# A graph network in four layers: the scores' R as two float32r rows, spread in one pass; both sides' scores from one product

## The chip, the cores and the metric

The kernel runs on one core of a Trainium2 chip. The metric is the device time of one execution, in microseconds (us). Before the change it was 3072.85 us, the median of three executions (3069.26 to 3073.18).

The engines are named as in the profile: PE (matrix products; PEld is its weight load), DVE (vector), ACT (scalar functions), POOL (here: gathers by index), SP (issues transfers).

## The reference

Four layers over N = 3327 nodes of width D = 512; each reads a normed copy of x and adds its result to x. Layers 0, 2 and 3 are graph attention with H = 8 heads of F = 64, layer 1 takes the mean over neighbours.

```python
h = jnp.maximum(_layernorm(x, axis=-1), 0.0);  x = x + L0(h, adj)   # likewise L1, L2, L3

def attention(h, adj, W, a):             # L3; L0 adds a batch norm and relu, L2 has own a1, a2
    hp = jnp.einsum('nd,hdf->hnf', h, W)
    f_src = jnp.einsum('hnf,hf->hn', hp, a_src)
    f_dst = jnp.einsum('hnf,hf->hn', hp, a_dst)
    e = jax.nn.leaky_relu(f_src[:, :, None] + f_dst[:, None, :], 0.2)
    att = jax.nn.softmax(jnp.where(adj[None] > 0, e, -9e15), axis=-1)
    return elu(jnp.einsum('hij,hjf->hif', att, hp))       # heads side by side

def sage(h, adj, ...):                   # L1
    agg = (adj > 0) @ h / jnp.maximum(deg, 1.0)
    return relu(concat([h @ W_self + b, agg @ W_nb + b], -1) @ W_comb + b_comb)
```

The adjacency is sparse: an edge has a probability of about half a per cent, more for the first nodes.

The kernel uses that exp(leaky_relu(s + d)) is exp(d) times exp(0.2 s) times the larger of exp(0.8 s) and exp(-0.8 d). The middle factor falls out of the softmax. So a target node i needs only R(i) = exp(0.8 s_i), per head, scaled by a constant, and a neighbour j needs exp(d_j), exp(-0.8 d_j) and its row of hp.

## The kernel before

**Tiling.** The nodes are padded to 26 blocks of 128 rows. The targets are taken in 52 groups of 64 (GB), ordered by the nodes' index; each group has a list of its neighbours in chunks of 128: 22 chunks for the first group, 4 for the last, 359 in all (21 of the groups have five). Work of attention goes in units of up to three chunks (UNIT = 3), of the averaging layer in parts of two.

**Stages**, with their place in the profiled execution:
- 0 to 330 us: the lists are made from the adjacency, and beside them the projection of layer 0, block by block (`Projection.block`, L578-604). Here the scheduler chooses the order.
- 330 to 400: list transfers.
- 400 to 980: attention of layer 0, with products of weights for layer 1 beside it (fwx, bmean, fb).
- 980 to 1155: batch norm, layer 1's own products.
- 1155 to 1757: averaging (SAGE); beside it the projection of layer 2, by `Following`.
- 1757 to 2462: attention of layer 2; beside it the projection of layer 3, by `Following`.
- 2462 to 3068: attention of layer 3, with no projection.

**A projection** makes, for each block of 128 nodes: the transposed block hT; the scores s and d of all heads; hp = h W (wh). It leaves two things in memory: a row per node in `table` (V: exp(d) times hp and exp(d) itself, then exp(-0.8 d)), and R in `r_dram`, with the nodes along the row. WA holds the attention vectors already multiplied into W, for a side H = 8 columns: the first 8 for s, the next 8 for d. Before the change d comes from hT as the stationary operand (L708 in `Following`: 128 nodes by 8), and s from WA as the stationary operand (L710: 8 by 128 nodes), so that s comes out along the row. Each is four products, over the four parts of D.

`Following.rest` (L698-731) is a generator. Its steps for a block: transposes p_ps (L701) and hT by ACT (L704) | both score products p_sd (L708, L710), the exps of d (L713, L714), the copy of s out of PSUM (L716) | the clamp on DVE (L719), the products p_wh (L722) | the exp of R on ACT (L724), its transfer (L726), V's eight scalings (L730), the transfer of the table's rows (L731). `Following.tick` (L661) advances the first ready block by one step, and the blocks still in their norm by one each. A tick is called once per unit in attention, and once per pair of chunks in SAGE (L1320-1360). The tiles p_ps, p_sd and p_wh share one tag in PSUM, with two buffers during SAGE and one during attention 2 (`pb`).

**Attention** (`attend`, L1000-1125) has its order on PE, DVE and ACT written out by hand: each engine runs its instructions in the order of the program. For each group R's row is fetched two groups ahead (L1017-1020, a transfer of 512 values to one partition), and spread one group ahead: `spread` (L1023-1028) multiplies a column of ones with it, so that all 128 partitions have the 64 x 8 values (r_bc, one bank of PSUM). For each unit: DVE takes the larger of r_bc and the gathered exp(-0.8 d) (mx, L1096), DVE multiplies by the mask (wgt, L1103), the rows of the next unit are gathered (POOL, L995), `later()` runs a step of the endings of earlier groups and the tick (L1062), then at the start of a group the spread of the next, then PE's 8 products per chunk (facc, L1117). The ending of a group copies the sums (L1045), and scales the heads (rd L1049, fhp L1055); every second one finishes a block (fin_e, fin_x).

All data is float32, and a float32 product is issued as two records of matmul in the trace.

Of the kernel before, what the change touches and what calls it, by code (L numbers as in the profile page):

```python
# [22 lines left out]

F32 = mybir.dt.float32
BF16 = mybir.dt.bfloat16
I32 = mybir.dt.int32
I8 = mybir.dt.int8
U8 = mybir.dt.uint8
U16 = mybir.dt.uint16
AF = mybir.ActivationFunctionType  # L30
ALU = mybir.AluOpType
# [5 lines left out]
P = 128  # L37
H = 8
F = 64
D = H * F  # L40
KC = D // P
# [7 lines left out]
GB = 64  # L49
# [10 lines left out]
SMALL = 53.0  # L60
# [502 lines left out]
class Projection:  # L563
# [15 lines left out]
    def block(self, c):  # L579
        nc, pp, pps, WA, wl = self.tc.nc, self.pool, self.psum, self.WA, self.wl  # L580
        hT = self.norms.block(c, self.hs)
        wh = pps.tile([P, D], F32, name="wh_ps", tag="wh_ps", bufs=1)
        sd = pps.tile([P, BANK], F32, name="sd_ps", tag="sd_ps", bufs=1)
        for kc in range(KC):
            nc.tensor.matmul(sd[:, :H], hT[:, kc, :], WA[:, wl, kc, H:], start=(kc == 0), stop=(kc == KC - 1))
        for kc in range(KC):
            nc.tensor.matmul(sd[:H, P : 2 * P], WA[:, wl, kc, :H], hT[:, kc, :], start=(kc == 0), stop=(kc == KC - 1))
        for kc in range(KC):
            nc.tensor.matmul(wh, hT[:, kc, :], self.Wt[:, kc, :], start=(kc == 0), stop=(kc == KC - 1))  # L589
        row = pp.tile([P, ROW], F32, name="v_row", tag="v_row", bufs=3)  # L590
        V = row[:, : H * (F + 1)].rearrange("p (h f) -> p h f", f=F + 1)
        nc.scalar.activation(V[:, :, F : F + 1], sd[:, :H].rearrange("p (h o) -> p h o", o=1), AF.Exp)
        nc.scalar.activation(row[:, H * (F + 1) :], sd[:, :H], AF.Exp, scale=-0.8, bias=self.cs["down"])

        rr = pp.tile([H, P], F32, name="r_row", tag="r_row", bufs=2)
        nc.vector.tensor_scalar(rr, sd[:H, P : 2 * P], -SMALL, SMALL, ALU.max, ALU.min)
        nc.scalar.activation(rr, rr, AF.Exp, scale=0.8, bias=self.cs["down"][:H])
        n = P // GB
        nc.sync.dma_start(
            self.r_dram[c * n : (c + 1) * n, :, :].rearrange("g h i -> h g i"), rr.rearrange("h (g i) -> h g i", i=GB)  # L600
        )
        for h in range(H):
            nc.scalar.mul(V[:, h, 0:F], wh[:, h * F : (h + 1) * F], V[:, h, F : F + 1])
        nc.sync.dma_start(self.table[c * P : (c + 1) * P, :ROW], row.bitcast(I32))

# [36 lines left out]
    return step  # L642


class Following:


# [11 lines left out]
        self.early.append(self.norm(c, xt))  # L659

    def tick(self):  # L661
        if self.ready and next(self.ready[0], None) is None:
            self.ready.pop(0)
        for g in list(self.early):
            hx = next(g)
            if hx is not None:
                self.early.remove(g)
                self.ready.append(self.rest(*hx))
# [28 lines left out]
    def rest(self, c, hx):  # L697
        nc, pp, WA, wl = self.tc.nc, self.pool, self.WA, self.wl  # L698
        tp = self.psum.tile([P, KC, P], F32, name="p_ps", tag="p_ps", bufs=self.pb)
        for kc in range(KC):  # L700
            nc.tensor.transpose(tp[:, kc, :], hx[:, kc * P : (kc + 1) * P], self.cs["ident"])  # L701
        hT = pp.tile([P, KC, P], F32, name="hT", tag="hT", bufs=2)
        for kc in range(KC):
            nc.scalar.activation(hT[:, kc, :], tp[:, kc, :], AF.Relu, accum_out=self.hs[:, c, kc : kc + 1])  # L704
        yield True
        sd = self.psum.tile([P, BANK], F32, name="p_sd", tag="p_ps", bufs=self.pb)
        for kc in range(KC):
            nc.tensor.matmul(sd[:, :H], hT[:, kc, :], WA[:, wl, kc, H:], start=(kc == 0), stop=(kc == KC - 1))  # L708
        for kc in range(KC):
            nc.tensor.matmul(sd[:H, P : 2 * P], WA[:, wl, kc, :H], hT[:, kc, :], start=(kc == 0), stop=(kc == KC - 1))  # L710
        row = pp.tile([P, ROW], F32, name="v_row", tag="v_row", bufs=2)
        V = row[:, : H * (F + 1)].rearrange("p (h f) -> p h f", f=F + 1)
        nc.scalar.activation(V[:, :, F : F + 1], sd[:, :H].rearrange("p (h o) -> p h o", o=1), AF.Exp)  # L713
        nc.scalar.activation(row[:, H * (F + 1) :], sd[:, :H], AF.Exp, scale=-0.8, bias=self.cs["down"])  # L714
        rr = pp.tile([H, P], F32, name="r_row", tag="r_row", bufs=2)
        nc.scalar.copy(rr, sd[:H, P : 2 * P])  # L716
        yield True

        nc.vector.tensor_scalar(rr, rr, -SMALL, SMALL, ALU.max, ALU.min)  # L719
        wh = self.psum.tile([P, D], F32, name="p_wh", tag="p_ps", bufs=self.pb)  # L720
        for kc in range(KC):
            nc.tensor.matmul(wh, hT[:, kc, :], self.Wt[:, kc, :], start=(kc == 0), stop=(kc == KC - 1))  # L722
        yield True
        nc.scalar.activation(rr, rr, AF.Exp, scale=0.8, bias=self.cs["down"][:H])  # L724
        n = P // GB
        nc.sync.dma_start(  # L726
            self.r_dram[c * n : (c + 1) * n, :, :].rearrange("g h i -> h g i"), rr.rearrange("h (g i) -> h g i", i=GB)
        )
        for h in range(H):
            nc.scalar.mul(V[:, h, 0:F], wh[:, h * F : (h + 1) * F], V[:, h, F : F + 1])  # L730
        nc.sync.dma_start(self.table[c * P : (c + 1) * P, :ROW], row.bitcast(I32))  # L731
        yield None


# [232 lines left out]
def sparse(ctx: ExitStack, tc: tile.TileContext, t: dict, out: bass.AP, WA, ls, cs, idx, rdeg, first):  # L967
# [5 lines left out]
    nc = tc.nc  # L973
# [9 lines left out]
    dram = ctx.enter_context(tc.tile_pool(name="fdram", bufs=1, space=DRAM))  # L983
# [4 lines left out]
    ones = cs["ones"]  # L988
# [11 lines left out]
    def attend(layer, table, r_dram, finish, tick=lambda: None, home=None):  # L1000
# [11 lines left out]
        with tc.tile_pool(name=f"fatt{layer}", bufs=2) as ap, tc.tile_pool(  # L1012
            name=f"facc_ps{layer}", bufs=2, space=PSUM
        ) as aps, tc.manual_schedule(engines={ET.PE, ET.DVE, ET.Activation}):
            rows, rrs, rbs, accs, ends = {}, {}, {}, {}, []

            def fetch(g):  # L1017
                if g < ls.G:
                    rr = ap.tile([1, H * GB], F32, name="r_one", tag="r_one", bufs=3)
                    nc.sync.dma_start(rr, r_dram[g : g + 1, :, :].rearrange("g h i -> g (h i)"))  # L1020
                    rrs[g] = rr

            def spread(g):  # L1023


                if g < ls.G:
                    rb = aps.tile([P, H * GB], F32, name="r_bc", tag="r_bc", bufs=2)
                    nc.tensor.matmul(rb, ones[0:1, :], rrs.pop(g), start=True, stop=True)  # L1028
                    rbs[g] = rb.rearrange("p (h i) -> p h i", i=GB)

            def ending(g, hps={}):
# [59 lines left out]
            for i, (g, k0, n, begins, stops) in enumerate(units):  # L1091
# [20 lines left out]
                for k in range(n):  # L1112
                    f, l = begins and k == 0, stops and k == n - 1
                    for q in range(hq):
                        for v in range(PG):
                            h = q * PG + v
# [12 lines left out]
    def following(lx, layer, wl, W, pb=1):  # L1129

        table = dram.tile([NP, ROW], I32, name=f"table{layer}")
        r_dram = dram.tile([ls.G, H, GB], F32, name=f"r_dram{layer}")
        pp = lx.enter_context(tc.tile_pool(name=f"fproj{layer}", bufs=1))
        pps = lx.enter_context(tc.tile_pool(name=f"fproj_ps{layer}", bufs=1, space=PSUM))
        return Following(tc, cs, N, wl, W, WA, table, r_dram, pp, pps, pb)
# [24 lines left out]
    with ExitStack() as mx:  # L1160
# [180 lines left out]
        for i, (b, _, begins, stops) in enumerate(parts):  # L1341
# [4 lines left out]
            for r, u, k, m, z in loaded.pop(i):  # L1346
# [3 lines left out]
                g = b * PG + u  # L1350
# [17 lines left out]
def gnn_stack(tc: tile.TileContext, t: dict, out: bass.AP):  # L1368
    with ExitStack() as ctx:

        tc.nc.scalar.preload_act_table_set("natural_log_exp_and_others")
        WA, ok = products(ctx, tc, t)
        N, NP = out.shape[0], t["x"].shape[0]
        ls = Lists(NP)
        cs = constants(ctx, tc, N)
        kp = ctx.enter_context(tc.tile_pool(name="first", bufs=1))
        ldram = ctx.enter_context(tc.tile_pool(name="first_dram", bufs=1, space=DRAM))

        table = ldram.tile([NP, ROW + NP // WB // 2], I32, name="table0")
        r_dram = ldram.tile([ls.G, H, GB], F32, name="r_dram0")  # L1380
        idx = kp.tile([P, ls.n], I32, name="idx")
        rdeg = kp.tile([P, NP // P], F32, name="rdeg")
        with tc.tile_pool(name="fproj0", bufs=1) as pp, tc.tile_pool(name="fproj_ps0", bufs=1, space=PSUM) as pps:
            p = Projection(tc, cs, N, 0, t["x"], t["L0_gnn_W"], WA, table, r_dram, pp, pps, hb=1)
            lists(tc, t, ls, cs, N, ok, table, p, idx, rdeg)
        small = tc.nc.values_load(ok[0:1, 0:1], min_val=0, max_val=1, skip_runtime_bounds_check_because="a product of comparisons, 0 or 1")
        with tc.If(small > 0) as branch:
            sparse(tc, t, out, WA, ls, cs, idx, rdeg, (table, r_dram))
        with branch.Else():
            general(tc, t, out)  # L1390
# [60 lines left out]
```

## Time and profile before

| | us |
|---|---|
| median of three executions | 3072.85 |
| the profiled execution's own time | 3070.05 |
| its span, first to last instruction | 3067.8 |
| lists and projection of layer 0 (with the list transfers) | 400 |
| attention 0 | 580 |
| batch norm, own products | 175 |
| SAGE with projection 2 | 602 |
| attention 2 with projection 3 | 705 |
| attention 3 | 606 |

The spreads cost PE 66.0, 65.3 and 84.5 us in attention 0, 2 and 3, where the granted clock of PE is 0.79, 0.76 and 0.63 of the full. The score products cost it 56.4 us in SAGE and 83.5 us in attention 2.

How to read it: the page gives the busy time of each engine over the whole span; a window gives the same for a stretch. The chain is the sequence of work that ended last, followed backwards; a line's share of it is the time in which nothing but this work held the end. "Issue" in it is time in which an engine waited for nothing that the profile shows. In rows of groups, "out<-in" names the tiles, x is the number of records, then busy us and mean ns, then the idle time ahead of the group's instructions and what ended it.

### The profile page before, as it was taken

To read this page: it belongs to the slowest core of one execution; us is meant where nothing else is said; L and a number is where in the kernel's file an instruction comes from. 1 tells how busy PE (TensorE), PEld (TensorE's weight loads), DVE (VectorE), ACT (ScalarE), POOL (GpSimd) and SP (SyncE) were. 2 spreads that over 40 slices of the span, in tenths; PEclk is the share of its full clock that TensorE was granted. 3 is DMA by queue.
4 is the path that set the end of the run, shared out by engine and by line. 5 is a ranking of instruction groups with operands and counts; after the bars stand their busy time and mean duration, and the time that the engine had idled before them with its cause. 6 is when DMAs were issued, how large, how long until landed. Compare 5 with 4: busy or idle time off the path is not lost.

```text
span 3067.8 us, 55727 instructions
## 1 busy us (share of the span) xinstructions
PE 2324.5 (76%) x22046; PEld 1434.3 (47%) x22046; DVE 1781.0 (58%) x2077; ACT 1162.7 (38%) x4117; POOL 1375.4 (45%) x1462
## 2 busy tenths in 40 slices
PE   2888157877777797788888857888998857778876
PEld 1555034555554342333333345555665445555654
DVE  7434867787786840000111077777766457887886
ACT  3775012233334321344444402444666601222343
POOL 0000055566553026666554266555444155665653
PEclk9888678886777898889999867887877766675666
DMA  7671067777664455666666366566655256666774
GB/s 284 242 266 58 11 221 236 218 242 210 201 196 145 168 178 172 192 205 218 192 194 185 105 177 190 177 184 193 183 172 175 72 170 185 187 196 194 200 198 131
DMA packets 186641, 561.55 MB, mean 183 GB/s; under 512 B 35386, under 2 KB 40322, under 8 KB 183045
## 3 DMA queue, kind: packets, MB, share of 16 engines
q0 software_dynamic: 114880, 404.47, 45.2%
q1 hardware_dynamic: 70918, 153.04, 14.2%
q8 instruction: 177, 2.90, 0.4%
q14 instruction: 92, 0.75, 0.1%
q10 hardware_dynamic: 574, 0.39, 0.0%
HBM read 498.42 MB, written 59.36 MB: 182 GB/s over the span
## 4 chain that ended last, share of the span: by engine, by line
PE 63%; issue 13%; ACT 5%; DVE 2%; another core or an unknown queue 2%; DMA 1%; POOL 0%; DVEq 0%; SPq 0%; ACTq 0%; POOLq 0%
PE facc L1117 30%; PE p_wh L722 7%; PE r_bc L1028 6%; PE sage_acc L1352 5%; PE n_ps L1301 3%; PE p_sd L710 2%; PE p_sd L708 2%; PE s_ps L1276 2%; PE fwx_ps L1194 1%; PE bmean_ps L1204 1%; PE p_ps L701 1%; ACT v_row L730 1%; PE a_ps L1295 1%; DMA fWc<-in_L_gnn_W_comb 1%
## 5 line engine op out<-in xcount | busy, mean ns | idle before, releaser
L995 POOL DMA_INDIRECT rows<-table,idx x1077 | 1027.7, 954 | 1222.8 <-PE facc L1117 350.9
L1117 PE MATMUL facc<-rows,wgt 128*64 128x65 f32 x17232 | 958.0, 270 | 371.5 <-issue 358.0
L1117 PEld LDWEIGHTS facc<-rows,wgt 128*64 128x64 f32 x17232 | 820.8, 179 | 668.7 <-issue 588.7
L1103 DVE TENSOR_TENSOR wgt<-mx,mask 128x1536 f32<-128x1536 f32 (+1 forms) x405 | 638.4, 1576 | 168.2 <-PE facc L1117 78.6
L1096 DVE TENSOR_TENSOR mx<-r_bc,rows 128x1536 f32<-128x1536 f32 (+1 forms) x405 | 639.5, 1579 | 161.1 <-PE facc L1117 68.4
L995 POOL DMA_INDIRECT z_rows<-h_dram,idx x359 | 341.2, 950 | 395.2 <-ACT hT L1273 138.8
L1055 ACT ACTIVATE fhp<-sums,rd 64x64 f32<-64x64 f32 x832 | 219.7, 334 | 145.5 <-DVE rd L1049 71.3
L1028 PE MATMUL r_bc<-r_one,fones 1*128 1x512 f32 x312 | 217.8, 783 | 16.6 <-DMA r_one<-r_dram 8.6
L1352 PE MATMUL sage_acc<-z_rows,z_mask 128*64 128x512 f32 x718 | 210.6, 641 | 14.0 <-issue 7.7
L722 PE MATMUL p_wh<-fWt,hT 128*128 128x512 f32 x416 | 214.5, 661 | 2.0 <-ACT r_row L716 1.8
L1088 ACT ACTIVATE mask<-on 128x192 uint8<-128x192 uint16 (+1 forms) x135 | 46.5, 344 | 445.4 <-DVE on L1082 181.8
L1045 ACT COPY sums<-facc 128x260 f32<-128x260 f32 x156 | 57.5, 369 | 407.6 <-PE facc L1117 289.3
L719 DVE TENSOR_SCALAR r_row<-r_row 8x128 f32<-8x128 f32 x52 | 11.7, 226 | 307.3 <-ACT r_row L716 224.0
L1306 DVE TENSOR_TENSOR s_o<-n_ps,bn_y 128x512 f32<-128x512 f32 x26 | 17.9, 688 | 206.9 <-PE n_ps L1301 190.3
L722 PEld LDWEIGHTS p_wh<-fWt,hT 128*128 128x128 f32 x416 | 84.6, 215 | 107.1 <-issue 101.3
L589 PE MATMUL wh_ps<-fWt,hT 128*128 128x512 f32 x208 | 121.3, 709 | 2.8 <-ACT hT L776 2.8
L730 ACT ACTIVATE v_row<-p_wh,v_row 128x64 f32<-128x64 f32 x416 | 89.7, 321 | 73.8 <-PE p_wh L722 72.5
L1055 ACT ACTIVATE bn_y<-sums,rd 64x64 f32<-64x64 f32 x416 | 109.5, 333 | 2.4 <-DVE rd L1049 0.5
L1301 PE MATMUL n_ps<-fWx,aT 128*128 128x512 f32 x208 | 106.1, 649 | 5.1 <-ACT aT L1297 4.9
L1352 PEld LDWEIGHTS sage_acc<-z_rows,z_mask 128*64 128x64 f32 x718 | 51.7, 142 | 119.9 <-issue 105.6
L1276 PE MATMUL s_ps<-fWx,hT 128*128 128x512 f32 x208 | 96.1, 616 | 9.0 <-ACT hT L1273 9.0
L713 ACT ACTIVATE v_row<-p_sd 128x8 f32<-128x8 f32 x52 | 9.6, 184 | 240.5 <-PE p_sd L710 107.3
(196 smaller groups left out, 2291.3 us busy)
## 6 DMA issues: line engine op xcount, KB each, us to landing
adj_i<-in_adj SPq DMA_DIRECT2D x26, 1664.0 KB
table<-v_row SPq DMA_DIRECT2D x78, 264.0 KB
rows<-table,idx POOLq DMA_INDIRECT x1077
fin_x<-fx SPq DMA_DIRECT2D x52, 256.0 KB
ln_x<-in_x SPq DMA_DIRECT2D x26, 256.0 KB
bn_x<-in_x SPq DMA_DIRECT2D x13, 512.0 KB
fx<-bn_x SPq DMA_DIRECT2D x13, 512.0 KB
fsage_x<-fx SPq DMA_DIRECT2D x26, 256.0 KB
```

Source lines behind the costliest of these rows:

```text
L589: nc.tensor.matmul(wh, hT[:, kc, :], self.Wt[:, kc, :], start=(kc == 0), stop=(kc == KC - 1))
L722: nc.tensor.matmul(wh, hT[:, kc, :], self.Wt[:, kc, :], start=(kc == 0), stop=(kc == KC - 1))
L730: nc.scalar.mul(V[:, h, 0:F], wh[:, h * F : (h + 1) * F], V[:, h, F : F + 1])
L995: nc.gpsimd.indirect_dma_start(out=dst, out_offset=None, in_=src[:, :], in_offset=bass.IndirectOffsetOnAxis(ap=idx[:, k : k + 1], axis=0))
L1028: nc.tensor.matmul(rb, ones[0:1, :], rrs.pop(g), start=True, stop=True)
L1055: nc.scalar.mul(hp[o0 : o0 + GB, h * F : (h + 1) * F], sm[mine, q, 0:F], rd[mine, q, :])
L1096: nc.vector.tensor_tensor(mx[:, :n], rbs[g].unsqueeze(1).to_broadcast(full), gt[:, :n, H * (F + 1) : ROW].unsqueeze(3).to_broadcast(full), ...
L1103: nc.vector.tensor_tensor(wt[:, :n], mx[:, :n], mk.unsqueeze(2).to_broadcast(full), ALU.mult)
L1117: nc.tensor.matmul(accs[g][v * GB : (v + 1) * GB, q * (F + 1) : (q + 1) * (F + 1)], wt[:, k, h, :], gt[:, k, h * (F + 1) : (h + 1) * (F + 1)],
L1276: nc.tensor.matmul(ps, hT[:, kc, :], Wx[:, 0, kc, :], start=(kc == 0), stop=(kc == KC - 1))
L1301: nc.tensor.matmul(ps, aT[:, kc, :], Wx[:, 1, kc, :], start=(kc == 0), stop=(kc == KC - 1))
L1352: nc.tensor.matmul(acc[u * GB : (u + 1) * GB, :], m, z, start=f, stop=l)
```

## The change

R is kept as two float32r rows instead of one float32 row: the value rounded to float32r, and the difference of the value to it (`halves`, new). A product of two rows of ones with the two, in float32r, adds them up again[...].

Both sides' scores come from one product with hT stationary and all 16 columns of WA, so s now comes out as a column per head, nodes along the partitions. R is computed there as 128 x 8, split into halves 128 x 16, transposed on PE to 16 x 128 (p_tr), copied out and sent to `r_dram`, which has two rows per head. `rest` gets six steps instead of four, and `tick` advances up to two steps where two blocks are ready.

```diff
@@ Projection.block
-            nc.tensor.matmul(sd[:, :H], hT[:, kc, :], WA[:, wl, kc, H:], ...)
-        for kc in range(KC):
-            nc.tensor.matmul(sd[:H, P : 2 * P], WA[:, wl, kc, :H], hT[:, kc, :], ...)
+            nc.tensor.matmul(sd[:, : 2 * H], hT[:, kc, :], WA[:, wl, kc, :], ...)
...
-        nc.vector.tensor_scalar(rr, sd[:H, P : 2 * P], -SMALL, SMALL, ALU.max, ALU.min)
-        nc.scalar.activation(rr, rr, AF.Exp, scale=0.8, bias=self.cs["down"][:H])
+        sf = pp.tile([P, H], F32, name="s_col", tag="s_col", bufs=2)
+        nc.vector.tensor_scalar(sf, sd[:, :H], -SMALL, SMALL, ALU.max, ALU.min)
+        rs = halves(nc, pp, self.cs, sf)
+        nc.tensor.transpose(sd[: 2 * H, P : 2 * P], rs(), self.cs["ident"])
+        rr = pp.tile([2 * H, P], F32, name="r_row", tag="r_row", bufs=2)
+        nc.scalar.copy(rr, sd[: 2 * H, P : 2 * P])
...
+def halves(nc, pool, cs, sf):
+    rf = pool.tile([P, H], F32, name="r_full", tag="r_full", bufs=2)
+    rs = pool.tile([P, 2, H], F32, name="r_half", tag="r_half", bufs=2)
+    nc.scalar.activation(rf, sf, AF.Exp, scale=0.8, bias=cs["down"])
+    nc.scalar.copy(rs.bitcast(F32R)[:, 0, :], rf)
+
+    def other():
+        nc.vector.tensor_tensor(rs.bitcast(F32R)[:, 1, :], rf, rs[:, 0, :], ALU.subtract)
+        return rs.rearrange("p t h -> p (t h)")
+    return other
@@ Following.tick
-        if self.ready and next(self.ready[0], None) is None:
-            self.ready.pop(0)
+        for _ in range(min(2, len(self.ready))):
+            while self.ready and next(self.ready[0]) is None:
+                self.ready.pop(0)
@@ Following.rest
-            nc.tensor.matmul(sd[:, :H], hT[:, kc, :], WA[:, wl, kc, H:], ...)
-        for kc in range(KC):
-            nc.tensor.matmul(sd[:H, P : 2 * P], WA[:, wl, kc, :H], hT[:, kc, :], ...)
+            nc.tensor.matmul(sd[:, : 2 * H], hT[:, kc, :], WA[:, wl, kc, :], ...)
...
-        nc.scalar.copy(rr, sd[:H, P : 2 * P])
+        sf = pp.tile([P, H], F32, name="s_col", tag="s_col", bufs=2)
+        nc.scalar.copy(sf, sd[:, :H])
         yield True
-        nc.vector.tensor_scalar(rr, rr, -SMALL, SMALL, ALU.max, ALU.min)
+        nc.vector.tensor_scalar(sf, sf, -SMALL, SMALL, ALU.max, ALU.min)
...
-        nc.scalar.activation(rr, rr, AF.Exp, scale=0.8, bias=self.cs["down"][:H])
...
+        rs = halves(nc, pp, self.cs, sf)
         for h in range(H):
             nc.scalar.mul(V[:, h, 0:F], wh[:, h * F : (h + 1) * F], V[:, h, F : F + 1])
         nc.sync.dma_start(self.table[c * P : (c + 1) * P, :ROW], row.bitcast(I32))
+        yield True
+        tr = self.psum.tile([2 * H, P], F32, name="p_tr", tag="p_ps", bufs=self.pb)
+        nc.tensor.transpose(tr, rs(), self.cs["ident"])
+        yield True
+        rr = pp.tile([2 * H, P], F32, name="r_row", tag="r_row", bufs=2)
+        nc.scalar.copy(rr, tr)
...
@@ attend: fetch, spread
-                    rr = ap.tile([1, H * GB], F32, name="r_one", tag="r_one", bufs=3)
-                    nc.sync.dma_start(rr, r_dram[g : g + 1, :, :].rearrange("g h i -> g (h i)"))
+                    rr = ap.tile([2, H * GB], F32, name="r_two", tag="r_two", bufs=3)
+                    nc.sync.dma_start(rr, r_dram[g, :, :, :].rearrange("t h i -> t (h i)"))
...
-                    nc.tensor.matmul(rb, ones[0:1, :], rrs.pop(g), start=True, stop=True)
+                    nc.tensor.matmul(rb, ones[0:2, :].bitcast(F32R), rrs.pop(g).bitcast(F32R), start=True, stop=True)
```

## The prediction

> **What bounds the kernel now.** First the page: busy time, the clock strip, the instruction queue, the chain that ended last.
>
> ```profile
> PE 2324.5 (76%) x22046; PEld 1434.3 (47%) x22046; DVE 1781.0 (58%) x2077; ACT 1162.7 (38%) x4117; POOL 1375.4 (45%) x1462
> PEclk9888678886777898889999867887877766675666
> q8 instruction: 177, 2.90, 0.4%
> PE 63%; issue 13%; ACT 5%; DVE 2%; another core or an unknown queue 2%; DMA 1%; POOL 0%; DVEq 0%; SPq 0%; ACTq 0%; POOLq 0%
> PE facc L1117 30%; PE p_wh L722 7%; PE r_bc L1028 6%; PE sage_acc L1352 5%; PE n_ps L1301 3%; PE p_sd L710 2%; PE p_sd L708 2%; PE s_ps L1276 2%; PE fwx_ps L1194 1%; PE bmean_ps L1204 1%; PE p_ps L701 1%; ACT v_row L730 1%; PE a_ps L1295 1%; DMA fWc<-in_L_gnn_W_comb 1%
> ```
>
> PE carries the chain, 13% of it is "issue", and the two products to be changed stand on it: r_bc 6%, L710 2%. Next the windows by stage (span, PE busy, PEld, DVE, ACT, POOL, clock, DMA): attend 0, SAGE, attend 2, attend 3.
>
> ```profile
> 400.00:980.00 580.00, 444.10 (x5964) 296.62 (x5966) 455.54 (x458) 172.96 (x598) 335.84 (x355) 0.79 0.70 216
> 1155.00:1757.00 602.00, 497.19 (x1761) 207.42 (x1760) 58.49 (x160) 240.72 (x992) 320.41 (x337) 0.90 0.59 183
> 1757.00:2462.00 705.00, 567.47 (x6584) 389.23 (x6584) 480.93 (x480) 335.41 (x1275) 343.78 (x359) 0.76 0.58 169
> 2462.00:3068.00 606.00, 444.76 (x5848) 336.34 (x5848) 462.02 (x374) 161.28 (x520) 343.93 (x359) 0.63 0.65 184
> ```
>
> The reader is to see how little the length of an attention stage follows PE's work. Attend 0 has about 94 us of products that attend 3 lacks (fwx, bmean, fb) and is 26 us shorter, at a higher clock. Attend 2 has about 210 us that attend 3 lacks (p_wh 107, p_sd 83, p_ps 21) and is 99 us longer: 47% got through. What is nearly the same is the rate: matmuls plus weight loads over the stage, 20.6, 18.7 and 19.3 a microsecond. Then the chain cut to SAGE, attend 2 and attend 3, in this order.
>
> ```profile
> by line: PE sage_acc L1352 23.9%; PE n_ps L1301 17.2%; PE p_wh L722 15.1%; another core or an unknown queue 6.9%; PE p_sd L710 4.3%; ACT v_row L730 4.1%; PE p_sd L708 3.8%; issue 3.8%; PE a_ps L1295 3.3%; PE p_ps L701 3.0%; ACT ln_j L685 2.
> by line: PE facc L1117 37.9%; PE p_wh L722 15.9%; issue 15.5%; PE r_bc L1028 7.8%; PE p_sd L710 5.9%; PE p_sd L708 5.8%; PE p_ps L701 2.7%; ACT v_row L730 1.5%; DMA rows<-table,idx 0.9%; ACT hT L704 0.9%; POOL rows L995 0.8%; DVE mx L1096 0
> by line: PE facc L1117 59.7%; issue 21.4%; PE r_bc L1028 12.8%; ACT fhp L1055 1.0%; DMA rows<-table,idx 0.8%; DVE mx L1096 0.5%; POOL rows L995 0.3%; DMA table<-mean 0.3%; ACT fin_x L1146 0.2%; DVEq L1096 0.1%; DVE fin_x L1148 0.1%; DVE fin
> ```
>
> Issue is a fifth of attend 3 and 3.8% of SAGE. A PE timeline of attend 3 shows what it is:
>
> ```profile
> 2480.11 0.27 PE L1117 MATMUL facc<-rows,wgt 128*64 128x65 f32 x1 [1.05 <-issue]
> 2482.94 0.27 PE L1117 MATMUL facc<-rows,wgt 128*64 128x65 f32 x1 [1.83 <-issue]
> 2485.05 0.27 PE L1117 MATMUL facc<-rows,wgt 128*64 128x65 f32 x1 [1.84 <-issue]
> 2487.16 0.27 PE L1117 MATMUL facc<-rows,wgt 128*64 128x65 f32 x1 [1.83 <-issue]
> 2489.95 2.33 PE L1117 MATMUL facc<-rows,wgt 128*64 128x65 f32 x38 [0.34 <-issue]
> ```
>
> The operands are there, and still the products come singly; then 38 of them run in 2.33 us. Queue q8 moved 2.90 MB in 177 packets, 16 KB each; 44,092 PE records over 177 is 249 a packet, and in all three attention stages a packet comes about every 12 us, which is 20 to 21 records a microsecond. My reading: PE's instruction supply sets much of the pace of the attention stages, and execution that is saved there turns partly into waiting for instructions. SAGE, at 5.9 records a microsecond, is bound by execution.
>
> **What the Trainium skill says.** "Runtime: NRT & Kernel Launch", Instruction fetch mechanics: an engine's instructions come in 16 KiB blocks of 256 over a queue of its own, prefetched, the cost "mostly hidden". The packets agree; that it is hidden doesn't: 13% of the chain. "FP8 and Floating Point Precision", TensorE Precision Notes: a true FP32 product takes four passes. The trace agrees: p_wh's four products are eight records in 3.6 us at the best, a pass of 512 columns 0.23 us. "TensorE: Matmul & The Clock Gate", Part 1: the clock is gated by activity; the strip shows 0.6 to 0.9, and one spread takes 1.12 us or 2.07 us.
>
> **The change part by part.** The groups:
>
> ```profile
> L1028 PE MATMUL r_bc<-r_one,fones 1*128 1x512 f32 x312 | 217.8, 783 | 16.6 <-DMA r_one<-r_dram 8.6 <-issue 3.4 <-PE facc L1117 2.3
> L710 PE MATMUL p_sd<-hT,WA 128*8 128x128 f32 x416 | 71.7, 329 | 2.7 <-issue 2.5
> L708 PE MATMUL p_sd<-WA,hT 128*128 128x8 f32 x416 | 71.8, 287 | 20.5 <-issue 11.0 <-ACT hT L704 8.7 <-ACT fhp L1055 0.3
> L724 ACT ACTIVATE r_row<-r_row,fdown 8x128 f32<-8x128 f32 x52 | 20.6, 396 | 4.1 <-DVE r_row L719 2.3 <-issue 1.2
> ```
>
> *Spread.* 156 products of four passes (two records each) become one-pass products of two rows. No trace here shows a float32r product. Below: a quarter, 0.28 us for 1.12; above: unchanged. I take the quarter, since the code asks for one read of each value. Execution saved by stage: three quarters of 66, 65 and 84 us, that is 50, 49 and 63. Records saved: 52 pairs a stage, 104.
>
> *Scores.* L710 goes: in SAGE 26 us and in attend 2 41.6 us of the chain, 8 pairs a block. L708 gets 16 columns for 8; its weight load of 128 columns (0.24 us) sets its pace, so nothing. L587 goes too in projection 0 (35.3 us).
>
> *R as columns.* A block trades a copy 8x128 (0.24), a clamp and an exp (0.40) for a copy, a clamp and an exp of 128x8 (0.18 like L713), a rounding copy (about 0.2), a subtraction on DVE (about 0.15), a transpose (0.33 to 0.66 with its load) and a copy 16x128 (0.24): ACT +0.3, DVE +0.1 us. ACT is at 48% and DVE at 68% of attend 2. The write of R is twice the bytes in 256-byte pieces, on SP, which is nearly idle; R is ready one or two ticks later and read only a stage later. The last block alone sees it: +1.5 us for each of two drains, +3.
>
> *Tick.* The chain of a block has six steps instead of four, and two blocks' worth of ticks may go two steps at once. In the changed program's order, in attend 2 the transposes p_ps stand directly ahead of p_sd 17 times, 14 more than before. There p_sd waits for ACT's hT: four activations of 0.278 us, each with a read of its sum beside the next, about 1.25 us with ACT free; behind p_sd wait r_bc and the facc products of that unit, which mostly wait for DVE's wgt anyway. About half hidden: 17 x 1.6 less what hides, +8 with the transposes of R.
>
> Sum, against the profiled execution's own 3070.05 us:
> - Attend 0 and attend 3: 104 records each less, at 20 a microsecond 5 us, and of 50 and 63 us of saved execution some 13%, 7 us: −12 each. What is late next is the supply and DVE's mx and wgt (about 13.7 us of each 16.4 us pair of groups).
> - Attend 2: 104 + 416 records less, 52 more for R's transposes: 468, at 20 is 23 us; execution 91 us less, of which 15% beyond that, 14; ticks +8: −29. Straight from the 47% the same 91 us give −43, plus 8, −35.
> - SAGE: −26 from L710, transposes and their waits +7: −19.
> - Projection 0: 35 us of PE go, in a stage where PE is 68% busy, but the list steps of DVE (about 6.7 us each) stand later by up to two against the last blocks: −20 to +13, taken at nothing.
> - Drains +3.
>
> −12 −12 −29 −19 +3 = −69: 3001. The median shown is 2.8 above the profiled execution: 3004.
>
> **The rivals.** *B: execution binds.* Then the stages give all they save: r_bc 146 us (three quarters of its 195 on the chain), L710 67 less 10. 203 us gives 2870; at two thirds, as DVE's 13.7 of 16.4 us would cap it, 2937. For it: PE 63% of the chain and every share of r_bc on it. Against it: attend 0 beside attend 3.
>
> *C: slower, by one round trip in attend 2.* At the 17 places PE stands still from p_ps until ACT has written hT. ACT runs in order, and ahead of hT may stand fin_e and fin_x (0.61 + 0.71), sums (0.38) and fhp (2.14): up to 5.1 us with hT's 1.25. Behind p_sd waits the spread of the next group, then mx of it on DVE. 17 x 5.1 is 87 us for the +8 in the sum, and with 8 more of V's scaling (1.74 us) before some p_tr the result is +18, 3091. It decides once the stop costs more than 4.5 us a place, since the rest gives 77 in all. For it: ACT's hT already waits 20 us on p_ps, and L708 8.7 us on hT. Against: a tick is 4 us, and ACT is half idle.
>
> *D: float32r takes as many passes as before,* and the change doesn't do what it says: only L710 counts, −19 −15 +3, 3041.
>
> **How the numbers follow.** Chances: mine 0.52, B 0.24, C 0.17, D 0.07. About 0.2% (6 us) can be told from no change here. Mine reaches from 2955 to 3060, with projection 0's −20 to +13 and 0 to 30% of saved execution; 0.05 of it falls within 0.2% and 0.03 above. C gives 0.14 slower, 0.02 the same, 0.01 faster; D 0.06 and 0.01; B all faster. Faster 0.75, same 0.07, slower 0.18. The range, 2905 to 3085, leaves out B's full size and C's worse half.
>
> **What would show it.** r_bc in one record of 0.25 to 0.3 us with the clock full (D: 1 us). Attend 0 and 3 shorter by 5 to 20 us each, with "issue" a larger share of their chains, q8's packets still 12 us apart: right; shorter by 40 or more: B. In attend 2, p_sd waiting for hT about 1.5 us a place; 5 or more is C. SAGE shorter by some 20 us. I am wrong if the rate of PE records rises above 22 a microsecond over a whole stage, since then supply was no bound.

## The result: nothing gained, 0.2% lost

The changed kernel takes 3079.02 us (median of 20 executions, 3065.67 to 3094.15), the kernel before 3073.3 (20, 3065.46 to 3083.55): a ratio of 1.0023, 95% interval 1.0008 to 1.0037. Forecast were 3004 us.

The first lines of the page of the changed kernel: busy time of the engines, PE's clock, the chain by engine and by line.

```profile
PE 2192.5 (71%) x21344; PEld 1384.1 (45%) x21344; DVE 1786.2 (58%) x2155; ACT 1179.8 (38%) x4273; POOL 1370.4 (44%) x1462
PEclk9787568887776898788999866888888677666666
PE 53%; issue 15%; ACT 8%; another core or an unknown queue 5%; DVE 3%; DMA 2%; POOL 0%; DVEq 0%; SPq 0%; ACTq 0%
PE facc L1144 27%; PE p_wh L742 6%; PE sage_acc L1379 5%; PE n_ps L1328 3%; PE r_bc L1055 2%; PE s_ps L1303 2%; PE p_sd L729 2%; ACT v_row L746 2%; PE fwx_ps L1221 1%; ACT fhp L1082 1%; PE bmean_ps L1231 1%; PE p_ps L722 1%; ACT hT L725 1%; DVE mx L1123 1%
```

PE did 132 us less work (2324.5 to 2192.5), as was meant: r_bc fell from 6% to 2% of the chain, and L710 is gone. In their place stand issue (13 to 15%), ACT (5 to 8%) and waits without a known releaser (2 to 5%). The groups of the changed instructions (records, busy us, mean ns, idle before and its releasers):

```profile
L1055 PE MATMUL r_bc<-r_two,fones 2*128 2x512 f32 x156 | 95.6, 616 | 13.4 <-DMA r_two<-r_dram 8.8 <-DVE idx L975 2.0 <-issue 1.4
L729 PE MATMUL p_sd<-WA,hT 128*128 128x16 f32 x416 | 74.4, 302 | 67.9 <-ACT hT L725 53.8 <-issue 13.4 <-ACT fhp L1082 0.4
L750 PE MATMUL p_tr<-fident,r_half 128*16 128x128 f32 x52 | 14.6, 280 | 29.9 <-DVE r_half L659 10.0 <-remote 7.8 <-ACT v_row L746 5.5
```

The spread is one record instead of two and costs 95.6 us instead of 217.8. The score product costs as much with 16 columns as with 8 (74.4 and 71.8). But PE stands idle ahead of it for 67.9 us, 53.8 of them for hT; before, L708 stood 20.5 us, 8.7 of them for hT.

By stage, from the first to the last product of facc or sage_acc (each from one profiled execution, so a few us can be scatter; the profiled changed one took 3084.05 us, its span is 3081.7):

| us | before | changed |
|---|---|---|
| start of attention 0 | 410.0 | 421.0 |
| attention 0 | 570.4 | 570.3 |
| SAGE | 611.6 | 615.1 |
| attention 2 | 645.1 | 636.0 |
| end of attention 2 to attention 3 | 61.9 | 68.6 |
| attention 3 | 570.5 | 572.1 |

The windows of the changed kernel for attention 2 and attention 3 (span, PE, PEld, DVE, ACT, POOL, clock, DMA), then the chain of attention 3 by line, before and changed, over the stage as in the table:

```profile
1784.00:2420.00 636.00, 480.41 (x6273) 356.97 (x6275) 473.95 (x485) 312.50 (x1214) 332.62 (x350) 0.77 0.61 180
2489.00:3061.00 572.00, 399.95 (x5794) 326.69 (x5792) 455.90 (x368) 156.18 (x504) 333.37 (x350) 0.68 0.65 189
```

```profile
by line: PE facc L1117 63.3%; issue 22.4%; PE r_bc L1028 13.6%; ACT fhp L1055 0.5%; DVE mx L1096 0.2%; ACT fin_e L1144 0.1%; ACT fin_x L1146 0.1%; ACT sums L1045 0.1%; DVE rd L1049 0.0%; DVE wgt L1103 0.0%
by line: PE facc L1144 63.6%; issue 29.4%; PE r_bc L1055 5.0%; DVE mx L1123 0.7%; DVE wgt L1130 0.5%; ACT fhp L1082 0.5%; ACT fin_e L1171 0.1%; ACT fin_x L1173 0.1%; ACT sums L1072 0.1%; DVE rd L1076 0.1%; DVEq L1130 0.0%
```

In attention 3 r_bc fell from 13.6% to 5.0% of the chain, 49 us, and issue rose from 22.4% to 29.4%, 41 us: most of what was saved came back as issue, and the stage is 2 us longer.

The kernel before takes 2621 to 2629 us in four of the sets of runs below and 3048 in one, near the 3073 of the result, and the record names the same chip for a set of each kind, so that what makes the difference stays open: every run is set beside the kernel before of its own set, and "2620" and "3050" name the two cases from here on.

### The profile page after: what moved, and what is told of

Its sections match the earlier page's. It is cut to its first block, busy times and chain, and to the rows that moved or that the text cites. A ratio compares the mean times of both kernels' runs of the same rounds, so it can differ in the third digit from the quotient of the medians.

```text
span 3081.7 us, 54523 instructions
## 1 busy us (share of the span) xinstructions
PE 2192.5 (71%) x21344; PEld 1384.1 (45%) x21344; DVE 1786.2 (58%) x2155; ACT 1179.8 (38%) x4273; POOL 1370.4 (44%) x1462
## 4 chain that ended last, share of the span: by engine, by line
PE 53%; issue 15%; ACT 8%; another core or an unknown queue 5%; DVE 3%; DMA 2%; POOL 0%; DVEq 0%; SPq 0%; ACTq 0%
PE facc L1144 27%; PE p_wh L742 6%; PE sage_acc L1379 5%; PE n_ps L1328 3%; PE r_bc L1055 2%; PE s_ps L1303 2%; PE p_sd L729 2%; ACT v_row L746 2%; PE fwx_ps L1221 1%; ACT fhp L1082 1%; PE bmean_ps L1231 1%; PE p_ps L722 1%; ACT hT L725 1%; DVE mx L1123 1%
## 5 line engine op out<-in xcount | busy, mean ns | idle before, releaser
L1144 PE MATMUL facc<-rows,wgt 128*64 128x65 f32 x17232 | 980.6, 269 | 434.2 <-issue 384.2
L1144 PEld LDWEIGHTS facc<-rows,wgt 128*64 128x64 f32 x17232 | 830.5, 177 | 650.3 <-issue 556.0
L1379 PE MATMUL sage_acc<-z_rows,z_mask 128*64 128x512 f32 x718 | 230.3, 657 | 7.0 <-DMA z_rows<-h_dram,idx 4.4
L742 PE MATMUL p_wh<-fWt,hT 128*128 128x512 f32 x416 | 226.4, 692 | 2.1 <-ACT s_col L736 1.4
L739 DVE TENSOR_SCALAR s_col<-s_col 128x8 f32<-128x8 f32 x52 | 9.2, 176 | 324.4 <-ACT s_col L736 185.4
L589 PE MATMUL wh_ps<-fWt,hT 128*128 128x512 f32 x208 | 142.2, 816 | 17.2 <-ACT hT L803 15.4
L729 PE MATMUL p_sd<-WA,hT 128*128 128x16 f32 x416 | 74.4, 302 | 67.9 <-ACT hT L725 53.8
L729 PEld LDWEIGHTS p_sd<-WA,hT 128*128 128x128 f32 x416 | 71.2, 243 | 104.4 <-ACT hT L725 69.5
L1055 PE MATMUL r_bc<-r_two,fones 2*128 2x512 f32 x156 | 95.6, 616 | 13.4 <-DMA r_two<-r_dram 8.8
```

The source lines that it names most:

```text
L729: nc.tensor.matmul(sd[:, : 2 * H], hT[:, kc, :], WA[:, wl, kc, :], start=(kc == 0), stop=(kc == KC - 1))
L1055: nc.tensor.matmul(rb, ones[0:2, :].bitcast(F32R), rrs.pop(g).bitcast(F32R), start=True, stop=True)
L1144: nc.tensor.matmul(accs[g][v * GB : (v + 1) * GB, q * (F + 1) : (q + 1) * (F + 1)], wt[:, k, h, :], gt[:, k, h * (F + 1) : (h + 1) * (F + 1)],
L1379: nc.tensor.matmul(acc[u * GB : (u + 1) * GB, :], m, z, start=f, stop=l)
```

## The experiments

**Is it the supply of instructions, PE's work, or neither?** Four kernels, all made from the kernel before.

```diff
 spread, e1                       # and i1
-    nc.tensor.matmul(rb, ones[0:1, :], rrs.pop(g), start=True, stop=True)
+    rr = rrs.pop(g)
+    for _ in range(2):
+        nc.tensor.matmul(rb, ones[0:1, :], rr, start=True, stop=True)
 spread, e2: after the one spread
+    for _ in range(16):
+        nc.tensor.matmul(rb[0:64, 0:8], ones[0:1, 0:64], rr[:, 0:8], start=True, stop=True)
 facc, e3, where layer == 3       # and i2
-    wt[:, k, h, :], gt[:, k, h * (F + 1) : (h + 1) * (F + 1)]
+    upper(wt[:, k, h, :]), upper(gt[:, k, h * (F + 1) : (h + 1) * (F + 1)])
 attend, e4, where layer == 3: mx is written to wgt's tile
-    nc.vector.tensor_tensor(wt[:, :n], mx[:, :n], mk.unsqueeze(2).to_broadcast(full), ALU.mult)
```

> The kernel before, with every spread issued twice into the same tile (156 more float32 products of 512 columns: four passes, two records each, the same values). Supply theory (the rate at which TensorE's instructions arrive, 20 to 21 records a microsecond, sets the attention stages): only 4 more records a group, so at most +10 us a stage, +0 to +30 in all. Execution theory: +1.1 to 1.6 us a group, +57 to +85 us a stage, +195 in all. Vector theory (DVE's chain of mx and wgt with its waits is the pace): within 10 us a stage.

> The kernel before, with 16 more products of 1 row by 8 columns after every spread, writing the same values into its first 8 columns (64 more records a group, hardly any work). Supply theory: 64 records at 20.8 a microsecond are 3.1 us a group, +160 us a stage, +480 in all. Execution theory: at the pace of facc in a burst, 80 records with their loads in 2.55 us, 32 are 1.0 us a group, +53 us a stage, +160 in all, less than the doubled spread costs. Vector theory: within 40 us a stage.

> The kernel before, with facc of attention 3 on the upper 16 bits of each value, as bfloat16 (one pass and one record a product instead of four passes and two records; the rest of the value is left out of these products). Supply theory: half the records, so attention 3 falls from 570 us until DVE's 456 us with its waits bind, 470 to 510. Execution theory: about the same, 470 to 510, and with the clock lower. Vector theory: attention 3 stays at 560 to 575.

> The kernel before, with the product by the mask left out in attention 3 (mx is written straight where wgt was, so non-neighbours are not masked there): DVE does 213 us less. Supply and execution theory: attention 3 stays within 20 us of 570. Vector theory: it is shorter by 100 to 200 us.

The kernel before took 2628.77 us here. Measured (one execution each; stages as in the table above):

| us | all | attention 0 | attention 2 | attention 3 |
|---|---|---|---|---|
| e1 spread twice | 2651.93 | 476.1 | 520.3 | 473.3 |
| e2 tiny products | 2790.93 | 502.1 | 601.5 | 508.7 |
| e3 upper halves in attention 3 | 2630.11 | 471.3 | 503.0 | 471.3 |
| e4 no mask product in attention 3 | 2598.13 | 468.9 | 503.2 | 449.3 |

Attention 0 and 2 of e3 and e4 are those of the kernel before: 470 and 503. No profile of the kernel before was taken at 2620, so its attention 3 is put at 472: e3 changes nothing else and takes as long as it (2630.11 us, and 1.0008 when repeated as i2). e4 leaves the mask out, so its sums are not those of the reference; only its time is used. The windows of e2 (three attention stages), e3 and e4 (attention 3):

```profile
411.00:913.00 502.00, 486.03 (x7572) 378.43 (x7572) 450.59 (x455) 170.00 (x598) 329.23 (x347) 0.81 0.77 242
1594.00:2195.00 601.00, 569.69 (x8078) 448.19 (x8078) 471.53 (x462) 307.93 (x1170) 335.33 (x350) 0.82 0.65 190
2258.00:2767.00 509.00, 457.37 (x7444) 397.08 (x7444) 455.62 (x368) 152.42 (x501) 331.63 (x349) 0.72 0.72 212
```

```profile
2134.00:2606.00 472.00, 208.37 (x2972) 114.53 (x2972) 454.97 (x368) 151.87 (x501) 334.70 (x350) 0.50 0.78 228
```

```profile
2124.00:2573.00 449.00, 322.84 (x5840) 260.95 (x5840) 245.20 (x232) 150.96 (x499) 337.14 (x352) 0.77 0.81 241
```

Here 7572 matmuls and as many loads ran in 502 us: 30 records a microsecond. So 20 to 21 is no limit of PE's supply at 2620. Attention 3 doesn't become shorter there with half of PE's records (e3), so PE doesn't set it at all; it becomes 22 us shorter with 210 us less of DVE's work (e4, 455 to 245), so DVE sets it only by a little. What e4 is left with are the gathers, which wait for nearly nothing (waits of e4 in attention 3: us in total, times, longest):

```profile
POOL rows L995 <- issue: 72.2, 237, 0.3
POOL rows L995 <- PE facc L1118: 19.5, 64, 0.3
```

A gather takes 0.95 us and comes 0.30 after the one before; 359 of them are 449 us at that pace. In e4 they take 454, begun 9 us ahead of the stage, and its attention 3 is 449.3. No expectation had that. No run changed the gathers, so that they set the stage next is read from these waits. Attention 2, where the projection is added, does feel more work on PE (e1 +17 us, e2 +98). i1 and i2 are e1 and e3 again, meant for 3050, and they ran at 2620 as well.

> The kernel before with every spread issued twice, again, for a chip on which it takes near 3050 us. Held-back theory (there TensorE's records come at a rate of their own in attention 0 and 3, and its work counts little): attention 0 and 3 within 10 us of 565, with fewer than 150 steps of 0.7 us in attention 3, against 209. Execution theory: +57 to +85 us each. If the kernel before takes near 2620, this repeats the earlier run, +24 us in all.

> The kernel before with facc of attention 3 on the upper 16 bits of each value as bfloat16 (one record and one pass for two and four; the rest of the value is left out), again, for a chip on which the kernel before takes near 3050 us. Held-back theory: half the records, so attention 3 falls from 562 to about 471, where gathers and DVE hold it on the other chip; the ratio is 0.965 to 0.975. If something other than TensorE sets attention 3 on this chip (gathers or their landing): it stays above 550.

The kernel before took 2621.79 us (14 executions); the ratios are i1 1.0058 (1.0011 to 1.0105), i2 1.0008 (0.9991 to 1.0025), stages within 4 us of those of e1 and e3. Both repeat; whether PE's records set attention 3 at 3050 was not tried.

**Which part of the change loses?** The changed kernel, and each half alone: f2 keeps R as rows and both score products; f3 keeps the spread of one float32 row.

```diff
 f2, from the kernel before: rest, after the exp of R along the row
+    hi, lo = ...                                  # [H, P] each
+    nc.scalar.copy(hi.bitcast(F32R), rr)
...
+    yield True
+    nc.vector.tensor_tensor(lo.bitcast(F32R), rr, hi, ALU.subtract)
+    ...                                           # both to r_dram; fetch and spread as changed
 f3, from the changed kernel: halves gives the full R, one row, and spread is
-    nc.tensor.matmul(rb, ones[0:2, :].bitcast(F32R), rrs.pop(g).bitcast(F32R), start=True, stop=True)
+    nc.tensor.matmul(rb, ones[0:1, :], rrs.pop(g), start=True, stop=True)
```

> The changed kernel, unchanged. Theory of the held-back TensorE (on a chip where records come in steps of 0.7 us, work that is saved becomes such gaps): if the kernel before takes near 3070 here, within 0.4% of it; if it takes near 2620, attention 0 and 3 unchanged within 5 us, since gathers and DVE set them, and SAGE and attention 2 shorter by 10 to 30 us each, ratio 0.980 to 0.995. Rival (waits of p_sd for hT and the longer chain of a block eat the gain on any chip): ratio 0.997 to 1.005 on either.

> The float32r spread alone: R stays a row per head, its two parts are made there by a copy on ACT and a subtraction on DVE, both score products and the one step a tick stay. Held-back theory: near 3070, within 0.3%; near 2620, within 5 us in attention 0 and 3, up to 20 us less in attention 2, ratio 0.990 to 1.000. Execution theory: 0.95 on the slower chip.

> One product for both sides' scores alone, with R as columns, transposed, six steps and up to two a tick; the spread stays one float32 row in four passes. Held-back theory: near 3070, within 0.4%; near 2620, ratio 0.985 to 0.997 from SAGE and attention 2. Rival (waits for hT and the longer chain): 1.000 to 1.006, and attention 2 with p_sd waiting 2 us and more a block for hT.

The kernel before took 2621.57 us (7 executions), and the changed one is clearly slower here.

| | ratio (95%) | attention 0 | SAGE | attention 2 | to attention 3 | attention 3 |
|---|---|---|---|---|---|---|
| before (stages: e3) | 1 | 471.3 | 502.1 | 503.0 | 63.6 | about 472 |
| f1 changed | 1.0154 (1.0112 to 1.0196) | 466.3 | 501.3 | 536.2 | 65.6 | 474.3 |
| f2 spread alone | 1.0140 (1.0120 to 1.0161) | 467.3 | 502.6 | 495.6 | 102.4 | 472.1 |
| f3 scores alone | 1.0236 (1.0214 to 1.0259) | 468.9 | 501.0 | 557.3 | 66.7 | 472.5 |

"To attention 3" is the time from the end of attention 2 to its start. All expectations of a gain missed, and the rival was too mild as well: it had at most 1.005 for f1 and 1.006 for f3. The changed kernel loses 33 us in attention 2, and f3 54 there: the loss lies with the score side. The spread alone wins 7 us in attention 2 and 4 in attention 0; its 39 us ahead of attention 3 come from the way f2 is written, a fifth step in a block, for which a tick of one step hasn't the ticks, so that blocks are left for the drain. SAGE is untouched by any.

A timeline of PE in f1's attention 2 shows the loss (start, duration, line, in brackets the idle time and its releaser):

```profile
2037.19 0.28 PE L750 MATMUL p_tr<-fident,r_half 128*16 128x128 f32 x1
2037.40 1.15 PE L1144 MATMUL facc<-rows,wgt 128*64 128x65 f32 x32
2041.05 1.12 PE L722 MATMUL p_ps<-fident,ln_h 128*128 128x128 f32 x4 [2.50 <-ACT r_row L753]
2043.40 1.89 PE L729 MATMUL p_sd<-WA,hT 128*128 128x16 f32 x8 [1.23 <-ACT hT L725]
2045.22 0.79 PE L1055 MATMUL r_bc<-r_two,fones 2*128 2x512 f32 x1
```

and ACT in the same microseconds:

```profile
2038.91 0.81 ACT L715 ACTIVATE ln_h<-fin_x,ln_s,rs_y 128x512 f32<-128x512 f32 x1
2039.63 0.61 ACT L1171 ACTIVATE fin_e<-fhp 128x512 f32<-128x512 f32 x1
2040.15 0.71 ACT L1173 ACTIVATE fin_x<-fin_x,fless 128x512 f32<-128x512 f32 x1
2040.76 0.24 ACT L753 COPY r_row<-p_tr 16x128 f32<-16x128 f32 x1
2042.20 0.28 ACT L725 ACTIVATE hT<-p_ps 128x128 f32<-128x128 f32 x1 [1.21 <-PE p_ps L722]
```

p_tr was done at 2037.47. Its copy out of PSUM is issued a tick later, behind ln_h, fin_e and fin_x on ACT, and ends at 2041.00. Only then is the one buffer that p_ps, p_sd, p_wh and p_tr share free for the next block's transposes; and p_sd, in the same tick, waits for their copy hT. PE, with the next spread and facc queued behind, stands 3.7 us in this one tick. The spread stands directly behind p_sd at all 14 places where p_sd follows p_ps so. Over f1's attention 2 the waits of these three products (us in total, times, longest):

```profile
PE p_ps L722 <- ACT r_row L753: 27.9, 13, 2.5
PE p_sd L729 <- ACT hT L725: 17.6, 16, 1.2
PE p_tr L750 <- DVE rs_h L638: 8.9, 3, 3.5
PE p_tr L750 <- DVE r_half L659: 8.4, 5, 2.6
PE p_tr L750 <- ACT fhp L1082: 6.6, 3, 3.0
```

**Is the order of the steps the whole of the loss?** h1 is f2 with its last step in the tick of the next block's first; h2 (and j1) is the changed kernel with the copy in the step of the transpose, and that step in the tick of the next block's transposes; h3 is the changed kernel with the copy moved alone.

```diff
 h2, j1, from the changed kernel: tick            # h1: the same tick, on f2
-    for _ in range(min(2, len(self.ready))):
-        while self.ready and next(self.ready[0]) is None:
-            self.ready.pop(0)
+    while self.ready and next(self.ready[0]) is None:
+        self.ready.pop(0)
 h2, h3, j1: rest
     nc.tensor.transpose(tr, rs(), self.cs["ident"])
-    yield True
     rr = pp.tile([2 * H, P], F32, name="r_row", tag="r_row", bufs=2)
     nc.scalar.copy(rr, tr)
```

> The kernel before, unchanged, for its profile beside those of the changed kernel on the same chip. If it takes near 2620 us: attention 0 and 3 about 471 us, attention 2 about 503, no gaps of 0.7 us between TensorE's records. If near 3070: 570, 645, 570 and some 180 such gaps in attention 3.

> The float32r spread alone as before, but the last step of a block (subtraction and transfer) runs in the same tick as the first of the next, so that a block takes four ticks again and nothing is left for the drain. If the kernel before takes near 2620. Buffer theory (the gain is lost in the order of a block's steps on the one PSUM buffer, not in the float32r spread): attention 2 stays at 490 to 498, the end of attention 2 to attention 3 falls from 102 to 62 to 68 us, ratio 0.990 to 0.997. Rival (making and moving the second row costs as much as the single pass saves): ratio 1.000 to 1.006.

> The changed kernel with another order of steps: the transpose of R and its copy out come in one step, in the same tick as the next block's transposes, and a tick takes one step: four ticks a block, p_ps and p_sd never in one tick. If the kernel before takes near 2620. Buffer theory: p_sd waits for hT no more, p_ps for r_row under 1 us a block, p_tr for V little; attention 2 falls from 536 to 490 to 510, ratio 0.988 to 0.998. Rival (the longer chain of a block itself, or the lower clock with fewer passes): attention 2 stays over 525 and the ratio over 1.008.

> The changed kernel with its two steps a tick, and only the copy of R out of PSUM moved into the step of its transpose, ahead of other work on ACT. If the kernel before takes near 2620. Buffer theory, with its parts: the 28 us of p_ps waiting for r_row go for the most part, the 18 us of p_sd waiting for hT stay, attention 2 falls from 536 to 510 to 525, ratio 1.003 to 1.012. If the wait for hT is the main cause: within 8 us of 536.

> The changed kernel with the other order of steps (transpose, copy out and the next block's transposes in one tick, one step a tick), again, for a chip on which the kernel before takes near 2620 us. Buffer theory: attention 2 falls from the changed kernel's 536 to 490 to 510, ratio 0.988 to 0.999 to the kernel before. Rival (there DVE and gathers leave the longer chain of a block no room in any order): attention 2 over 525, ratio over 1.008.

h0 to h3 ran at 3050 (the kernel before 3048.39 us, 11 executions), so the sizes expected of them for 2620 don't apply, and only the directions can be read: h1 gains 0.7%, and its end of attention 2 to attention 3 is 63.8 us again; j1 ran at 2620 (2620.75, 15 executions).

| | median | ratio (95%) | attention 0 | SAGE | attention 2 | attention 3 |
|---|---|---|---|---|---|---|
| h0 before | 3023.76 (one) | | 565.7 | 595.3 | 628.3 | 562.2 |
| h1 spread alone | 3026.24 | 0.9932 (0.9912 to 0.9952) | 559.3 | 617.5 | 612.4 | 561.7 |
| h2 other order | 2993.88 | 0.9831 (0.9810 to 0.9853) | 562.4 | 604.8 | 594.2 | 561.0 |
| h3 copy moved | 3009.81 | 0.9892 (0.9855 to 0.9929) | 561.9 | 598.0 | 608.7 | 559.2 |
| j1 other order | 2617.48 | 0.9992 (0.9974 to 1.0010) | 466.5 | 495.6 | 502.8 | 473.0 |

With the same products and the same bytes, two lines of order turn 1.0023 (the result) into 0.983 at 3050 and 1.0154 (f1) into 0.999 at 2620; there attention 2 goes from 536 to 503. The changed kernel itself ran in neither of these two sets, so each pair compares ratios to the kernel before of its own set. The order is the loss, in both cases. j1's 0.9992 lies just past the losing end of the expected 0.988 to 0.999: the order brings attention 2 back to 503, not below it, and p_tr, now ahead of the next block's transposes, waits 42.5 us there for 23.9 in f1. The stages of single profiles scatter (SAGE 595 to 618 among these four; h0 is 25 us under its set's median, h2's profiled 3013.87 us are 20 over its own), so only attention 2, 34 us shorter in h2, stands out of them. At 3050 the wait of p_sd is what fell most; in attention 2 of the kernel before, of the changed one, and of h2:

```profile
PE p_sd L708 <- ACT hT L704: 1.1, 2, 0.6
```

```profile
PE p_sd L729 <- ACT hT L725: 41.9, 17, 4.1
```

```profile
PE p_sd L728 <- ACT hT L724: 3.1, 4, 0.9
```

Thirteen of the seventeen waits, 39.5 of the 41.9 us, stand where p_ps is directly ahead of p_sd: 3.0 us each, where f1 at 2620 has 1.23. There are 14 such places in the stage, and none in the kernel before; the other three that the prediction counted lie between attention 2 and 3, where the kernel before has them too. In h2 a part comes back at other products: PE's idle time ahead of p_ps is 25.3 us for the changed kernel's 16.1, ahead of p_tr 20.2 for 2.5. Of the two causes, the wait for the copy and the wait for hT, h3 doesn't say which counts how much: a block has a step less there, p_ps is directly ahead of p_sd at 7 places, and p_sd's wait fell too, to 10.7 us.

**What does the saved work turn into at 3050?** A timeline of PE in attention 3 of the changed kernel:

```profile
2946.74 0.34 PE L1144 MATMUL facc<-rows,wgt 128*64 128x65 f32 x3 [0.45 <-issue]
2947.48 0.36 PE L1144 MATMUL facc<-rows,wgt 128*64 128x65 f32 x5 [0.41 <-issue]
2948.95 0.28 PE L1144 MATMUL facc<-rows,wgt 128*64 128x65 f32 x2 [1.11 <-issue]
2949.65 0.27 PE L1144 MATMUL facc<-rows,wgt 128*64 128x65 f32 x1 [0.42 <-issue]
2950.37 0.46 PE L1144 MATMUL facc<-rows,wgt 128*64 128x65 f32 x2 [0.46 <-issue]
2951.82 2.69 PE L1144 MATMUL facc<-rows,wgt 128*64 128x65 f32 x44 [0.98 <-issue]
```

A few records, then nothing until a step of 0.7 us (or two) is full. To count them over attention 3, matmuls and weight loads are taken together; a run begins with a record that starts over 0.3 us after the one before it. Runs that begin 0.66 to 0.76 us after the run before are 201 in the kernel before and 240 in the changed one, 209 in h0, 275, 256 and 279 in h1, h2 and h3, and none in e3 and f1. So the cheaper spread comes with more such steps, and the stage keeps its length: h1 to h3 are 0.5 to 3 us shorter than h0 in attention 3, with r_bc at 32.6 us instead of 80.7 there (profile pair). What makes the steps stays open. The granted clock alone does not: the first three rows lie in a stretch in which it is 1.00 (2940 to 2949 us). Instructions that come late and another brake on PE both fit, and no run told them apart.

## Why the prediction was wrong

The profiled execution became 14 us longer where the sum has −69. Of the 83 us between them about 25 lie in attention 0 and 3, 23 in SAGE, 20 in attention 2, 11 in projection 0 and 4 in the drains.

- *The tick: this is the step that failed, and the one that the experiments isolate.* The prediction saw the place (p_ps directly ahead of p_sd in attention 2) and the mechanism (the stop until ACT has written hT, rival C), and put "+8" in the sum because the stop would be half hidden. Its own working doesn't give 8: half of 17 x 1.6 is 14 us, and the transposes of R come on top. The profile pair shows 41.9 us of waits, 3.0 a place, between the 1.6 of the prediction and the 5.1 of rival C. PE stood idle for all of it, with the spread of the next group directly behind p_sd. What the order costs as a whole: f1 against j1, which differ in nothing but the order, 33 us in attention 2; and h2's 0.983 beside the result's 1.0023, from two sets, about 2% of the whole. The profiles place some 25 us of that in attention 2 (−34 in h2 for −9); where the rest lies they don't show.
- *R as columns.* Costed right as work (p_tr 0.28 us, copy 0.24, subtraction 0.16), but not as a user of the buffer: it is the fourth tile in a PSUM buffer that holds one, and its copy was issued a tick after it, behind ACT's other work. The sum named p_tr's duration and not what waits for the buffer: p_ps, 27.9 us in f1. In the result's own profile that wait is 1.6 us in attention 2, so this part explains 2620 and not the result. Rival C had V's scaling ahead of p_tr, which was small.
- *Spread.* One record instead of two: right. A quarter of the time: wrong. The record takes 0.38, 0.50 and 0.79 us (shortest, median, longest) where there were two of 0.58, 0.69 and 1.22 each; 122 us were saved of 218, not 163. Rival D is out; whether the one record is one pass, no run shows.
- *Attention 0 and 3: −12 each.* −0.1 and +1.6 in the profile pair, −3 and −1 in h2 against h0, −5 and about +2 in f1. The reading that saved execution turns into issue holds; that 13% comes through doesn't show. The supply at 20 to 21 records a microsecond as the reason is not shown: e2 ran 30 a microsecond at 2620, where gathers and DVE set these stages instead. Nor do the packets of q8 tell of a supply: attention 3 has 48 in the kernel before, 46 in f1, 24 in e3 and 59 in e2, about one for each 250 records, so that "every 12 us" only says how fast PE went.
- *Attention 2: −29.* −9 in the profile pair; −34 in h2 against h0, once that stop is gone.
- *SAGE: −19.* +3.5 in the profile pair, −1 in f1, −6.5 in j1, with profiles that scatter by 20 us. L710's 26 us of the chain were not a saving: PE is as busy in the stage as before (508.0 us, then 507.4; at 2620 475.9 and 475.1), for as L710's time went, that of sage_acc's same products rose by 20 us in both cases, and p_tr brought 7. Why sage_acc's rose is not shown. PE's waits only moved: p_ps waits 38.8 us for 18.2, a_ps 20.9 for 57.9. At 2620 the kernel before already waits there for the gathers' rows (14.5% of its chain).
- *Projection 0: nothing, −20 to +13.* Attention 0 begins 11 us later in the profile pair, 413.5 in f1 against 410 to 417: not told from nothing. *Drains: +3.* +7 in the profile pair, +2 in f1. As forecast in kind.

Without the stop, and with attention 0, 3 and SAGE at the nothing that was measured, the sum would still have been a gain, −37 +3 = −34 us; h2 shows that a gain was there to have. That its 0.983 lies near the forecast 0.978 confirms no sum: against h0 its profile has −34 in attention 2, but −3, +9.5 and −1 where −12, −19 and −12 were forecast. Of the signs named, r_bc's record (0.25 to 0.3 us) and the shorter attention 0 and 3 and SAGE did not come; the larger share of issue did.

## What to carry to other kernels

When a step is moved or added on an engine that runs in the order of the program, price the stop by what is queued behind it and by how full the engine is on which it waits, and count for each shared buffer how many tiles use it and when the reader of each is issued. Put the copy out of a single buffer in the same step as the product that fills it, and never the reader of that copy's result behind it in the same tick. A share of the chain is not a saving: look for the next limit of that stage (at 2620 gathers at 1.25 us each, 449 us of a stage of 471) before it is taken off.

## What the runs showed of the hardware that was not expected

- At 3050 PE's records come in steps of 0.7 us, over 200 in attention 3, and at 2620 there is none. A gather takes 0.95 us and DVE's mx 1.76 (medians) in both. PE's granted clock differs: in SAGE it is 0.89 to 0.91 at 3050 and 0.98 or 0.99 at 2620.
- A float32r product of 2 rows by 512 columns is one record of 0.50 us (median), where a float32 product of one row is two records of 0.69. By busy time that is 95.6 us for 217.8, 2.3 times cheaper and not four.
- Gathers by index follow each other at 1.25 us (0.95 and 0.30) at best; with DVE's work nearly halved (e4) an attention stage of 359 of them takes 449 us.
